# Seven block products for values and output projection, with the values exchanged through DRAM

## The chip, the cores and the metric

The kernel runs on one core of a Trainium2 chip. The metric is device time in microseconds (us) of one execution, start to end; a lower number is better.

## The reference

One transformer layer over x of shape (1, 2048, 256), all in float32:

```python
xn = _layernorm(x, axis=-1)
# attention: 16 heads of 128
qkv = einsum('bsd,ed->bse', xn, Wqkv); q, k, v = heads of qkv
w = softmax(einsum('bqhd,bkhd->bhqk', q, k) * D ** -0.5)
out = einsum('bhqk,bkhd->bqhd', w, v).reshape(B, S, H * D)
attn = einsum('bse,de->bsd', out, Wout)
# feed-forward with weights quantized to -1, 0, 1
hidden = sigmoid(xn @ q(w1).T) * (xn @ q(w2).T)
x = x + attn + hidden @ q(w3).T
```

What the change touches is two of the projections: the values v (2048 rows by 256 inputs, 128 columns for each head) and the output product with Wout (256 outputs, 128 inputs for each head).

## The kernel before

**Blocks and steps.** After a lead-in (layer norm, feed-forward part, projections of the first heads) the work is a loop over 64 blocks, 16 heads times 4 query blocks of 512 rows. Block n has 4 steps t = 0 to 3. Two heads make a group g of 8 blocks; i = n mod 8 is the place of a block in its group. Blocks with i = 0 to 3 belong to the first head of the group, those with i = 4 to 7 to the second. There are 8 groups and so 7 passages from i = 7 of one group to i = 0 of the next.

**A step on TensorE (PE).** In each step PE makes the scores of 128 query rows, six steps ahead of the block whose values it weighs (`scores`, L548), then a projection product that is fitted in ("first product", `beside`), then one part r = t of the weighted sum (`weighted`, L695), then perhaps a "second product". Queries and keys of the head after next are made in steps t = 2 and 3 by `fast_product`/`fast_read` (L163, L180): a 2 x 2 block matrix product in seven block products instead of eight, after Strassen and Winograd. Steps t = 0 and 1 hold other products: for i = 0 to 3 the output projection of the group before (`o_product`, `o_read`), for i = 4 to 7 the values of the group after (`v_product`, `v_read`). Both are plain products of eight block products' worth. All these products use the one PSUM bank of pool `ps_m`, so that each must wait until VectorE (DVE) has read the one before it.

**The weighted sum.** The softmax weights p are exchanged between rows by DMA, turned by DVE (`transposed`, L641, line L646 of the profile) into the buffer R, and weighed by the values in seven products as well. For that GpSimd (POOL) subtracts slots of R (`differences`, L651): T1 in two halves a and b, T2 in two halves l and h, T3 in two halves, T4 in one piece twice as long. It also adds and subtracts quarters of the value tile (`v_combined`, L682) once for each head: two of these before the first block of the head, and two in its step 1, ahead of T4. T1b, T2l and T2h are needed by the weighted part r = 1, T3 and the last `v_combined` by r = 2, T4 by r = 3. In step t = 2 the DVE transposes for the next block overwrite a slot that T4 reads, and so wait for T4.

**Order.** There is no scheduler: each engine takes its instructions in the order in which the program writes them. POOL also starts the DMAs that are not part of the exchange, in that same order: the result of a block goes to DRAM at the start of the next block's step 0 (`put_away`, L766), the inverse sums go out in step 2 (`rd<-r`) and come back spread over the rows in step 1 (`spread`), and `between` (L872) fetches weights, stored results (`o_fetched`) and partial sums (`y_moved`), step by step.

Of the kernel before, what the change touches and what calls it, by code (L numbers as in the profile page):

```python
# [9 lines left out]
F32 = mybir.dt.float32  # L10
# [10 lines left out]
def layernorm_attention_bitffn_kernel(  # L21
# [18 lines left out]
    D = P  # L40
# [49 lines left out]
    def in_halves(out, lhs, rhs, start, stop, both=(True, True)):  # L90

        for c in range(2):
            if both[c]:
                nc.tensor.matmul(  # L94
                    out[c * HP : (c + 1) * HP], lhs[:, c * HP : (c + 1) * HP], rhs,
                    start=start, stop=stop, skip_group_check=True,
                )
# [47 lines left out]
    def weight_sums(h: int):  # L145
# [6 lines left out]
        nc.gpsimd.tensor_tensor(w[:, 3], wk[:, 1], w[:, 1], sub)  # L152
        ws[h] = w

    def x_sums(c: int):
        t = apool.tile([P, 4, QB], F32, tag=f"t{c}", name=f"t{c}", bufs=1)
        x00, x10 = (xnT[:, d, bass.ts(c, QB)] for d in range(KC))
        x01, x11 = (xnT[:, d, bass.ts(c + 1, QB)] for d in range(KC))
        for i, (a, b) in enumerate(((x01, x00), (x11, t[:, 0]), (x11, x01), (x10, t[:, 1]))):
            nc.gpsimd.tensor_tensor(t[:, i], a, b, ALU.subtract)  # L160
        ts[c] = t

    def fast_product(h: int, b: int, i: int, second: bool):  # L163

        c = b // 2 * 2
        wk, wq = (weights[h // G, i][:, :, bass.ts(h % G, D)] for i in "kq")
        w, t = ws[h], ts[c]
        x00, x10 = (xnT[:, d, bass.ts(c, QB)] for d in range(KC))
        x11 = xnT[:, 1, bass.ts(c + 1, QB)]
        lhs, rhs = {  # L170
            (0, 0): ((wk[:, 0], x00), (w[:, 1], t[:, 1])),
            (0, 1): ((w[:, 2], t[:, 2]), (wq[:, 1], t[:, 3])),
            (1, 0): ((w[:, 0], t[:, 0]), (w[:, 3], x11)),
            (1, 1): ((wk[:, 1], x10),),
        }[b % 2, i][second]
        pm = ps_m.tile([P, QB], F32, tag="m", name=f"pw{h}_{b}_{i}_{int(second)}")
        in_halves(pm, lhs, rhs, True, True)
        return pm

    def fast_read(h: int, b: int, i: int, second: bool, pm):  # L180
        c = b // 2 * 2
        if (b % 2, i) == (0, 0):
            if not second:
                if c == 0:
                    kTs[h] = kvpool.tile([P, S], F32, tag="kT", name=f"kT{h}")
                for j in range(2):
                    qTs[h, c + j] = kvpool.tile(
                        [P, QB], F32, tag="qT", name=f"qT{h}_{c + j}", bufs=NB + 2
                    )
        k0, k1 = (  # L190
            kTs[h].rearrange("p (j k r) -> p k j r", j=P // 32, r=32)[:, j * TB : (j + 1) * TB]
            for j in (c, c + 1)
        )
        q0, q1 = qTs[h, c], qTs[h, c + 1]
        pk = pm.rearrange("p (k j r) -> p k j r", j=P // 32, r=32)
        def q_sum(q, base):
            nc.vector.tensor_tensor(q, pm, base, ALU.add)

        def k_sum(k, base):
            nc.vector.tensor_tensor(k, pk, base, ALU.add)  # L200

        if (b % 2, i) == (0, 0):
            if not second:
                nc.vector.tensor_copy(k0, pk)
            else:
                k_sum(k1, k0)
        elif (b % 2, i) == (0, 1):
            if not second:
                nc.vector.tensor_tensor(
                    q1.rearrange("p (k j r) -> p k j r", j=P // 32, r=32), pk, k1, ALU.add  # L210
                )
            else:
                q_sum(q0, q1)
        elif (b % 2, i) == (1, 0):
            if not second:
                q_sum(q1, q1)
            k_sum(k1, k1)
        else:
            k_sum(k0, k0)
# [1 line left out]
    NV = NKT // 2  # L221

    osums = const.tile([P, 2, DM // P, QB], F32, tag="osums", name="osums")
    o3 = const.tile([P, G, QB], F32, tag="o3", name="o3")
    rinvs = [
        [const.tile([P, 32], F32, tag=f"r{i}{j}", name=f"r{i}{j}") for j in range(2)]
        for i in range(2)
# [30 lines left out]

    def v_product(g: int, m: int, second: bool):
        w = weights[g, "v"]
        pm = ps_m.tile([P, 2, G * D], F32, tag="m", name=f"pvw{g}_{m}")
        for j in range(2):
            for d in range(KC):
                in_halves(
                    pm[:, j], xnT[:, d, bass.ts(2 * m + j, P)], w[:, d], d == 0, d == KC - 1
                )
        return pm

    def v_read(g: int, m: int, second: bool, pm):
        for j in range(G):
            nc.vector.tensor_copy(
                v_tile(g * G + j)[:, 2 * m : 2 * m + 2], pm[:, :, bass.ts(j, D)]
            )

    ppool = ctx.enter_context(tc.tile_pool(name="ppool", bufs=2))
    front = ExitStack()
# [7 lines left out]
    ods = [  # L286
        [away.tile([P, G, QB], F32, tag=f"od{g}_{c}", name=f"od{g}_{c}") for c in range(NB)]
        for g in range(2)
    ]
    rds = [away.tile([P, 32], F32, tag=f"rd{i}", name=f"rd{i}") for i in range(2)]  # L290

# [481 lines left out]

    def o_fetched(g: int, b: int):
        nc.gpsimd.dma_start(o3, ods[g % 2][b])

    def y_moved(b: int, back: bool):
        y, yd = osums[:, (b + 1) % 2], yds[b]  # L780
        nc.gpsimd.dma_start(*((yd, y) if back else (y, yd)))

    def o_product(g: int, m: int, second: bool):
        w = weights[g, "o"]
        pm = ps_m.tile([P, QB], F32, tag="m", name=f"pow{g}_{m}")
        for i in range(G):
            in_halves(pm, w[:, i, bass.ts(m % 2, P)], o3[:, i], i == 0, i == G - 1)
        return pm

    def o_read(g: int, m: int, second: bool, pm):  # L790
        b, e = divmod(m, 2)
        y = osums[:, (b + 1) % 2, e]
        to = xnT[:, e, bass.ts(b, QB)] if g == H // G - 2 and b > 1 else y
        nc.vector.tensor_tensor(to, pm, y, ALU.add)

    sofar = {}

# [74 lines left out]
    def between(n: int, t: int):  # L872

        g, i = divmod(n, GB)
        last = NBK - NB

        if t == 1:
            if i == NB - 1 and g + 1 < H // G:
                load_weights(g + 1, "v", nc.gpsimd)
            elif i == GB - 1 and n < last or n == last - 1:  # L880
                load_weights(g, "o", nc.gpsimd)
        if g and i < NB:
            if t == 0 and i + 1 < NB:
                y_moved(i + 1, False)
            elif t == 1 and i + 1 < NB:
                o_fetched(g - 1, i + 1)
        elif n < last:
            if (i, t) == ((GB - 2, 2) if g else (GB - 1, 2)):
                y_moved(0, False)
            if (i, t) == (GB - 2, 3):  # L890
                o_fetched(g, 0)
        if n >= last - 1 and t == 2:
            b = n + 1 - last
            nc.gpsimd.dma_start(o3[:, b % 2], ods[(H - 2) // G % 2][b][:, 0])
        if (n, t) in ((last - 2, 3), (last - 1, 0)):
            fetched_back(n + 2 - last)
        if t == 0 and n in (last - 3, last - 2, last, last + 1):
            x_fetched((last - 3, last - 2, last, last + 1).index(n))

    behind = []  # L900
    with tc.manual_schedule():
        for u in range(-LEAD, (NBK - 1) * TB):
# [13 lines left out]
            if n >= NB and t < 2:  # L916
                i, j = divmod(i, NB)
                j = 2 * j + t
                if not i:
                    seven, hi = True, (g - 1, j)  # L920
                    product, read, twice = o_product, o_read, False
                elif g + 1 < H // G:
                    seven, hi = True, (g + 1, j)
                    product, read, twice = v_product, v_read, False
            pms = []

            def beside():
# [10 lines left out]
            if t == 0 and n >= 0:  # L938
                if 0 < n <= NBK - NB:
                    put_away(n - 1)  # L940
                differences(n, "T1b")
            elif t == 1 and n >= 0:
                differences(n, "T2h")
                differences(n, "T3b")
                spread(n)
                if blocks[n][1] == 0:
                    v_combined(blocks[n][0], 2)
                    v_combined(blocks[n][0], 3)
                differences(n, "T4")
            elif t == 3 and -1 <= n < NBK - 2:  # L950
                differences(n + 1, "T1a")
                if n % GB < NB <= n < NBK - NB - 2:
                    y_moved(n % GB, True)
                differences(n + 1, "T3a")
                if n >= 0 and blocks[n + 1][1] == 0:
                    v_combined(blocks[n + 1][0], 0)
                    v_combined(blocks[n + 1][0], 1)
            if more:
# [117 lines left out]
```

## Time and profile before

| | before |
|---|---|
| time, median of 3 runs | 2169.45 us (2166.16 to 2170.13) |
| time of the profiled execution | 2168.17 us |
| its span, first to last instruction | 2166.4 us |
| PE / DVE / ACT / POOL busy | 99% / 80% / 64% / 68% |
| granted TensorE clock | full speed throughout |
| DMA engines busy, mean rate | about 55%, 139 GB/s |

All line numbers in profile lines are those of the kernel before. `128*64` is a matmul on half the columns of the array; a float32 matmul shows as two records, so 16 records of 128x512 are four pairs of matmuls. A wait is put down to what ended last. Idle time of an engine that is not the bottleneck costs nothing.

### The profile page before, as it was taken

Reading aid. Unit: us, or ns where it says so; the run is one execution under the profiler, and the core shown is the slowest. Engines: PE = TensorE matmul, PEld = TensorE weight load, DVE = VectorE, ACT = ScalarE, POOL = GpSimd, SP = SyncE. Lnnn points to the kernel's source line nnn. Section 1 sums busy time; section 2 is a strip of 40 time slices with the busy share of each in tenths; the row PEclk is TensorE's granted clock in tenths of the full one; section 3 lists DMA queues with packets and bytes.
Section 4 is the critical chain, followed back from the end, with each engine's and each line's share of the span. In section 5 each row is a group of like instructions: output and inputs, shape, how many; then the busy total and the mean of one; then the engine's idle time right before and its main releaser. Section 6 shows DMA issues by size and latency. Waiting matters only on the chain. (4 is left out here: it accounts for less than half of the span.)

```text
span 2166.4 us, 41304 instructions
## 1 busy us (share of the span) xinstructions
PE 2153.8 (99%) x14074; PEld 1068.8 (49%) x14074; DVE 1726.9 (80%) x2338; ACT 1378.8 (64%) x2414; POOL 1474.5 (68%) x884
## 2 busy tenths in 40 slices
PE   9999999999999999999999999999999999999999
PEld 6744445444544444444444444544444444544456
DVE  6577887887887787887788788788788788788785
ACT  5587766666666666666666666666666666666673
POOL 0067767867667767767767776777766777676873
PEclk9999999999999999999999999999999999999999
DMA  2155555665556655566555654656555665556653
GB/s 94 40 117 140 130 121 126 166 178 128 115 141 165 162 129 125 143 171 154 124 133 144 169 149 110 145 154 169 135 116 135 169 162 132 117 145 176 178 143 98
DMA packets 180771, 300.65 MB, mean 139 GB/s; under 512 B 54416, under 2 KB 59920, under 8 KB 180560
## 3 DMA queue, kind: packets, MB, share of 16 engines
q1 hardware_dynamic: 127856, 175.21, 32.1%
q0 software_dynamic: 27152, 88.30, 16.6%
q10 hardware_dynamic: 25552, 34.51, 6.3%
q8 instruction: 111, 1.82, 0.4%
q14 instruction: 100, 0.82, 0.1%
HBM read 61.93 MB, written 34.54 MB: 45 GB/s over the span
## 5 line engine op out<-in xcount | busy, mean ns | idle before, releaser
L666 POOL TENSOR_TENSOR R<-R 128x1024 f32<-128x1024 f32 x441 | 1177.3, 2679 | 184.8 <-DVE R L646 103.9
L94 PE MATMUL s<-kT,qT 128*64 128x512 f32 x4000 | 901.1, 592 | 0.8 <-ACT p L578 0.8
L602 ACT COPY part<-p 32x512 f32<-32x512 f32 x1024 | 632.4, 618 | 380.9 <-issue 271.0
L568 DVE TENSOR_REDUCE mx<-s 128x1 f32<-128x1024 f32 x512 | 620.0, 1222 | 291.7 <-PE s L94 278.2
L578 ACT ACTIVATE p<-s,nm 128x1024 f32<-128x1024 f32 x512 | 567.0, 1112 | 212.4 <-PE pw L94 115.9
L646 DVE STREAM_TRANSPOSE R<-part 128x1024 f32<-128x1024 f32 x512 | 605.2, 1221 | 15.8 <-DMA part<-p 13.3
L94 PEld LDWEIGHTS s<-kT,qT 128*64 128x64 f32 x4000 | 288.2, 137 | 500.9 <-issue 440.8
L713 PE MATMUL av<-R,v 128*64 128x256 f32 x3728 | 528.5, 379 | 1.4 <-DVE oU L739 1.3
L713 PE MATMUL av<-R,st 128*64 128x256 f32 x3024 | 456.2, 379 | 2.5 <-DVE oU L739 1.6
L713 PEld LDWEIGHTS av<-R,v 128*64 128x64 f32 x3728 | 326.2, 137 | 141.0 <-issue 46.0
L713 PEld LDWEIGHTS av<-R,st 128*64 128x64 f32 x3024 | 283.5, 137 | 187.7 <-issue 55.2
L731 ACT COPY oU<-av 64x256 f32<-64x256 f32 x248 | 91.2, 368 | 121.2 <-PE av L713 118.7
L769 POOL DMA_DIRECT2D od<-oU x60 | 34.1, 568 | 184.8 <-DVE oU L743 184.5
L617 POOL DMA_DIRECT2D rd<-r x60 | 33.9, 564 | 169.0 <-DVE r L616 169.0
L739 DVE TENSOR_TENSOR oU<-av,oU 64x256 f32<-64x256 f32 x248 | 102.1, 412 | 44.7 <-ACT oU L731 42.1
L94 PE MATMUL pvw<-wv,xnT 128*64 128x256 f32 x896 | 106.2, 379 | 0.0
L94 PE MATMUL pow<-o,wo 128*64 128x512 f32 x448 | 105.6, 592 | 0.0
L578 ACT ACTIVATION_READ_ACCUMULATOR p<-s,nm 128x1 f32 x512 | 100.7, 197 | 0.0
L94 PEld LDWEIGHTS pvw<-wv,xnT 128*64 128x64 f32 x896 | 64.3, 137 | 56.3 <-issue 26.7
L94 PE MATMUL pw<-t,ws 128*64 128x512 f32 x336 | 86.4, 592 | 0.0
L200 DVE TENSOR_TENSOR kT<-pw,kT 128x512 f32<-128x512 f32 x112 | 76.9, 687 | 1.8
L160 POOL TENSOR_TENSOR t<-xnT 128x512 f32<-128x512 f32 x4 | 5.1, 1271 | 106.8 <-DMA part<-p 106.8
(146 smaller groups left out, 1295.1 us busy)
## 6 DMA issues: line engine op xcount, KB each, us to landing
part<-p SPq DMA_DIRECT2D x2560, 64.0 KB, 2.2
part<-p ACTq DMA_DIRECT2D x512, 64.0 KB, 2.2
oT<-rd POOLq DMA_DIRECT2D x60, 256.0 KB, 5.6
od<-oU POOLq DMA_DIRECT2D x60, 256.0 KB, 2.7
o<-od POOLq DMA_DIRECT2D x28, 512.0 KB, 4.4
osums<-yd POOLq DMA_DIRECT2D x28, 512.0 KB, 4.5
yd<-osums POOLq DMA_DIRECT2D x26, 512.0 KB, 3.4
yd<-yT SPq DMA_DIRECT2D x4, 512.0 KB, 2.6
```

What stands on the lines that cost most here:

```text
L94: nc.tensor.matmul(out[c * HP : (c + 1) * HP], lhs[:, c * HP : (c + 1) * HP], rhs, start=start, stop=stop, skip_group_check=True,)
L200: nc.vector.tensor_tensor(k, pk, base, ALU.add)
L568: nc.vector.tensor_reduce(mx[:, i : i + 1], s, AX.X, ALU.max)
L578: nc.scalar.activation(p, s, AF.Exp, bias=nm, scale=SCALE, accum_out=sums[n][:, t, i : i + 1],)
L602: nc.scalar.copy(*ends(j, j))
L617: nc.gpsimd.dma_start(rds[n % 2], riT)
L646: nc.vector.transpose(to[:, t % 2, 2 * i : 2 * i + 2], part.rearrange("p g (s c) -> p g s c", s=2),)
L666: nc.gpsimd.tensor_tensor(o, x, y, ALU.subtract)
L713: nc.tensor.matmul(av[i * HP : (i + 1) * HP, half], l[:, kk], moving(s, kk), start=start, stop=(k == units[r] - 1), skip_group_check=True,)
L731: nc.scalar.copy(u[op, oq], av[ap, half])
L739: nc.vector.tensor_tensor(u[p, q], av[p, half], u[p, q], ALU.add)
L769: nc.gpsimd.dma_start(ods[h // G % 2][b][:, h % G], oU)
```

## The change

The values of a group (both heads) and its output projection are now each made in seven block products for two query blocks, not eight. 

For the values the moving operand is x (with the sums in `ts` that queries and keys already use), so each product gives the values with their 128 columns on the partitions, and not the keys. The results are gathered in the value tile itself and then put in order: four DMAs for each half of each head write them to DRAM (`v_sent`), one DMA reads them back (`v_landed`) into a part of `xnT` that is not read any more, and two DVE transposes write the value tile (`v_transposed`). To free that part, the second pair of x blocks takes its two blocks in the other order (`pair`).

For the output the product that follows is added in PSUM onto the one before it; DVE adds the bank to the partial sums after each. `o3` has three slots, fetched one head and block at a time, with differences between them by POOL.

Weight sums for both are made by POOL (`v_sums`, `o_sums`). The products are split over the first and second product of steps 0 and 1. Only the core of the diff is shown.

```diff
+    def pair(c: int):
+        return (c, c + 1) if c == 0 else (c + 1, c)
...
-    o3 = const.tile([P, G, QB], F32, tag="o3", name="o3")
+    o3 = const.tile([P, 3, QB], F32, tag="o3", name="o3")
...
-    def v_product(g: int, m: int, second: bool):
-    def v_read(g: int, m: int, second: bool, pm):
...
+    def v_sums(g: int):
+        wv = weights[g, "v"]
+        sums_of(wv[:, :, D:], wv[:, :, :D], f"wvs{g}")
+    def sums_of(k, q, name: str):
+        w = wpool.tile([P, 4, D], F32, tag="wx", name=name)
+        nc.gpsimd.tensor_tensor(w[:, 0], q[:, 0], q[:, 1], ALU.add)
+        nc.gpsimd.tensor_tensor(w[:, 1], w[:, 0], k[:, 0], ALU.subtract)
+        nc.gpsimd.tensor_tensor(w[:, 2], k[:, 0], q[:, 0], ALU.subtract)
+        nc.gpsimd.tensor_tensor(w[:, 3], k[:, 1], w[:, 1], ALU.subtract)
+    def fast_v_product(g: int, m: int, second: bool):
...
+        lhs, rhs = (
+            ((wv[:, 0, D:], x00), (w[:, 1], t[:, 1])),
+            ((w[:, 2], t[:, 2]), (wv[:, 1, :D], t[:, 3])),
+            ((w[:, 0], t[:, 0]), (w[:, 3], x11)),
+            ((wv[:, 1, D:], x10),),
+        )[m][second]
+        pm = ps_m.tile([P, QB], F32, tag="m", name=f"pvw{g}_{half}_{m}_{int(second)}")
+        in_halves(pm, lhs, rhs, True, True)
+    def fast_v_read(g: int, m: int, second: bool, pm):
...
+        if (m, second) == (0, False):
+            nc.vector.tensor_copy(k0, pm)
+            return
+        todo = {
+            (0, True): ((k1, k0),), (1, False): ((q1, k1),), (1, True): ((q0, q1),),
+            (2, False): ((q1, q1), (k1, k1)), (2, True): ((k1, k1),), (3, False): ((k0, k0),),
+        }[m, second]
+        for o, i in todo:
+            nc.vector.tensor_tensor(o, pm, i, ALU.add)
+    def v_sent(h: int, half: int):
+        v = v_half(h, half).rearrange("p k d -> p (k d)")
+        vd = vds[h % G][half].rearrange("(j r) (q c) -> q r j c", r=32, c=S // 8)
+        for q in range(P // 32):
+            nc.gpsimd.dma_start(vd[q], v[bass.ts(q, 32)].rearrange("r (j c) -> r j c", c=S // 8))
+    def v_landed(h: int, half: int):
+        nc.gpsimd.dma_start(landing, vds[h % G][half])
+    def v_transposed(h: int, half: int):
...
+        for u in range(2):
+            nc.vector.transpose(v[:, 2 * u : 2 * u + 2], w[:, 2 * u : 2 * u + 2])
+    wxs, landing = {}, xnT[:, 0, QB : 3 * QB]
...
+    def o_fetched(g: int, b: int, head: int, slot: int):
+        nc.gpsimd.dma_start(o3[:, slot], ods[g % 2][b][:, head])
+    def o_difference(slot: int, x: int, y: int):
+        nc.gpsimd.tensor_tensor(o3[:, slot], o3[:, x], o3[:, y], ALU.subtract)
...
     def o_product(g: int, m: int, second: bool):
+        w, s = weights[g, "o"], wxs[f"wos{g}"]
+        lhs, slot, start = (
+            ((w[:, 0, :P], 0, True), (s[:, 1], 2, False)),
+            ((s[:, 0], 1, False),),
+            ((s[:, 2], 0, True), (w[:, 1, P:], 2, False)),
+            ((w[:, 1, :P], 1, True), (s[:, 3], 0, True)),
+        )[m % NB][second]
+        if start:
+            opms[g] = ps_m.tile([P, QB], F32, tag="m", name=f"pow{g}_{m}_{int(second)}")
+        in_halves(opms[g], lhs, o3[:, slot], start, True)
...
     def between(n: int, t: int):
+        v_steps = {
+            (5, 1): [(v_sent, 0, 0)],
+            (5, 3): [(v_transposed, 0, 0), (v_sent, 1, 0)],
+            (6, 1): [(v_landed, 1, 0)], (6, 2): [(v_transposed, 1, 0)],
+            (7, 1): [(v_sent, 0, 1)], (7, 3): [(v_transposed, 0, 1)],
+            (8, 1): [(v_sent, 1, 1)], (8, 3): [(v_landed, 1, 1)], (9, 1): [(v_transposed, 1, 1)],
+        }
...
+        if t == 3 and i == GB - 1 and g + 1 < H // G:
+            v_combined((g + 1) * G, 0)
+            v_combined((g + 1) * G, 1)
+        if n < last and (i, t) == (GB - 1, 3):
+            o_sums(g)
...
             elif t == 1 and n >= 0:
                 differences(n, "T2h")
+                if n >= NB and n % GB < NB and n % 2 == 0 and n < NBK - NB:
+                    o_difference(0, 2, 0)
                 differences(n, "T3b")
...
             elif t == 3 and -1 <= n < NBK - 2:
                 differences(n + 1, "T1a")
...
+                if n >= 0 and n % GB in (5, 7) and n // GB + 1 < H // G:
+                    v_landed((n // GB + 1) * G, n % GB // 2 - 2)
                 differences(n + 1, "T3a")
-                if n >= 0 and blocks[n + 1][1] == 0:
+                if n >= 0 and (n + 1) % GB == NB:
                     v_combined(blocks[n + 1][0], 0)
                     v_combined(blocks[n + 1][0], 1)
```

The keys (i, t) of `v_steps` are a block's place in its group (8 and 9 are places 0 and 1 of the group after) and its step; the numbers after a name are the head in the group and the half of the keys. `o_moved` (not shown) lays the fetches and differences of `o3` over the steps of i = 0 to 3: a partial sum for the second block of a pair is now fetched in step 0 of the first block, and the weights of the values are loaded in step 2 instead of step 1.

## The prediction

> **What bounds the kernel now.** I read the page's busy times first, then the groups by line, then the waits, then the timelines of PE, DVE and POOL around two places where the change puts its new steps.
>
> ```profile
> PE 2153.8 (99%) x14074; PEld 1068.8 (49%) x14074; DVE 1726.9 (80%) x2338; ACT 1378.8 (64%) x2414; POOL 1474.5 (68%) x884
> L94 PE MATMUL pvw<-wv,xnT 128*64 128x256 f32 x896 | 106.2, 379 | 0.0
> L94 PE MATMUL pow<-o,wo 128*64 128x512 f32 x448 | 105.6, 592 | 0.0
> ```
>
> PE has no gaps, so time is what PE is fed, as long as nobody makes it wait. The two groups are the products that the change cuts by an eighth. The others have slack that is cut up by waits:
>
> ```profile
> POOL od L769 <- DVE oU L743: 184.5, 59, 4.5
> POOL rd L617 <- DVE r L616: 169.0, 57, 13.0
> POOL R L666 <- DVE R L646: 103.9, 62, 3.6
> PE av L713 <- DVE oU L739: 2.9, 4, 1.1
> ```
>
> POOL's slack, about 3 us before `put_away` and 3 us before `rd`, takes extra work only if that work stands just there and is not itself late.
>
> **PE's saving.** The PE timeline around a passage from i=7 to i=0 (start, length, instruction):
>
> ```profile
> 1416.48 3.60 PE L94 MATMUL s<-kT,qT 128*64 128x512 f32 x16
> 1419.91 1.89 PE L94 MATMUL pow<-o,wo 128*64 128x512 f32 x8
> 1425.08 3.60 PE L94 MATMUL s<-kT,qT 128*64 128x512 f32 x16
> 1430.23 3.62 PE L713 MATMUL av<-R,st 128*64 128x256 f32 x32
> 1433.68 3.60 PE L94 MATMUL s<-kT,qT 128*64 128x512 f32 x16
> 1437.12 1.03 PE L94 MATMUL pw<-xnT,wk 128*64 128x512 f32 x4
> ```
>
> From start to start, 8 such records take 1.72 us and 4 take 0.86. Per group and kind there were 8 products of 1.72 (eight steps); now there are 14 half ones, so two times 0.86 go: in steps (0,1) and (2,1) for the output, (5,1) and (7,1) for the values, written (i,t). Saved: 2 x 2 x 7 x 0.86 = 24.0 us. All other steps keep their PE time.
>
> **DVE's added work.** Reads of the output go from 56 to 112 at 0.69 us, of the values from 112 copies at 0.42 to 112 instructions at 0.69: +39 and +30 us. 56 transposes of 512 columns, half of the L646 row (1.22 for 1024) plus a start, 0.65 each: +36. DVE goes to about 1832 us, still under PE. The reads lie in idle time: a second read comes at the start of the next step, where DVE waits 0.9 us (step 1) or 2.2 us (step 2) for scores; a double read in a first product leaves 1 us before PE's second product. Cost 0; without that cover each would cost up to 0.69.
>
> **POOL's added work.** 56 differences at 1.28 = 72 us, 56 weight sums at 0.45 = 25, and 182 more DMA issues at 0.57 = 104: about 200 us, POOL then at 77%. Most stands in the two waits above. The `o3` differences of i=1, 2 and 6 precede `put_away` (idle 4 us); the four `v_sent` issues (2.3 us) of (5,1), (7,1) precede `rd`, where POOL idles 3 to 4 us; `v_sums` pushes `put_away` by 0.9 us in i=3, where T2l then starts 0.1 us later. All 0. The later load of wv lands before its sums. The added wait in `o_product`, that a product adds to the bank that DVE has read, is the old one-bank wait: read done 1422.8, second product 1424.2. Two places are not free.
>
> **Place one: the passage i=7 to i=0** (7 times). POOL before:
>
> ```profile
> 1411.22 4.80 POOL L666 TENSOR_TENSOR R<-R 128x1024 f32<-128x1024 f32 x2 [1.64 <-DVE R L646]
> 1415.99 1.28 POOL L688 TENSOR_TENSOR st<-v 128x512 f32<-128x512 f32 x1
> 1419.94 0.57 POOL L769 DMA_DIRECT2D od<-oU  x1 [1.32 <-DVE oU L743]
> 1423.69 2.38 POOL L666 TENSOR_TENSOR R<-R 128x1024 f32<-128x1024 f32 x1 [0.78 <-PE av L713]
> 1426.01 0.56 POOL L781 DMA_DIRECT2D osums<-yd  x1
> 1434.49 4.53 POOL L666 TENSOR_TENSOR R<-R 128x2048 f32<-128x2048 f32 x1
> ```
>
> `st<-v` started at 1416.0. Now it reads values that `v_transposed` writes in the same step. That stands behind DVE's L646 pair (ends 1418.5) and needs `v_landed`, issued after T1a at 1413.6. At the 4.4 us of a like DMA that is 1418.0, so DVE is last: transposes done 1419.8. Then POOL in order, from rows: two `st` 2.64 to 1422.5; four weight sums 1.75 to 1424.3 (new); `put_away` 0.59; T1b 2.36; T2l 2.34 to 1429.6; the fetch of `osums` 0.57; T2h 2.35 to 1432.5; the new `o3` difference 1.28; T3b 2.35; `spread` 0.81; two `v_combined` 2.5 to 1439.4; T4 4.53 to 1443.96. It was at 1439.0.
>
> PE: its weighted part of step 1 would start at 1429.4 (product halved) and reach T2h's slices at 1431.1: waits 1.4. Part 2 needs the last `v_combined`: waits 1.0. Then DVE, in step 2, waits for T4: L646 from 1444.05 to 1446.3, L739 to 1447.2, the second read to 1447.9, so PE's first product of step 3 waits 0.7; two maxima and the scale to 1450.3, first read to 1451.0, second product 1451.1, end of step 3 at 1451.96. Unhindered it ends at 1449.16 - 0.86 = 1448.3. Loss 3.66 us (the waits of 1.4, 1.0, 0.7 and 0.6 lie inside it), x 7 = 25.6. The new fetch of `osums` for step 1 (landing 4.5) reaches DVE at 1434.6 against 1431.3, ahead of the T4 wait: adds nothing.
>
> **Place two: step (6,2).** `v_landed` of (6,1) stands behind T4, the weight sums of queries and a fetch. POOL's timeline, DVE's, and the list of DMA issues with the time to landing last:
>
> ```profile
> 1366.90 4.57 POOL L666 TENSOR_TENSOR R<-R 128x2048 f32<-128x2048 f32 x1
> 1372.79 0.46 POOL L152 TENSOR_TENSOR ws<-wk,ws 128x128 f32<-128x128 f32 x1
> ```
> ```profile
> 1375.40 2.37 DVE L646 STREAM_TRANSPOSE R<-part 128x1024 f32<-128x1024 f32 x2
> ```
> ```profile
> o<-od POOLq DMA_DIRECT2D x28, 512.0 KB, 4.4
> wq<-in_wqkvT_dram POOLq DMA_DIRECT2D x7, 256.0 KB, 5.6
> wk<-in_wqkvT_dram POOLq DMA_DIRECT2D x7, 256.0 KB, 4.3
> ```
>
> The transposes of (5,3) put `put_away` 1.2 us later, a fetch stands in step 0, so T4 ends near 1372.4, sums 1374.2, fetch 1374.75, then `v_landed`. DVE is free for its transposes at 1377.7. At 4.4 us it lands at 1379.15. It is queued right behind another fetch, as wq is and wk is not (5.6 against 4.3), half as long here, so up to 0.65 more. DVE then loses 1.5 to 2.1 us plus 1.3 of transposes, of which about 1.3 is slack; behind it are L739, the second read and the maxima, so PE's products of step 3 wait 1.5 to 2.1. I take 1.8 x 7 = 12.6; at the shortest `o` landing (3.3) it is 0.4 x 7 = 3, at the longest of `osums` (6.0) 3.1 x 7 = 22. At (5,3) landing and DVE meet (1418.0 against 1418.5) and PE has 0.1 us left: 0. At (9,1) DVE has 2.2 us: 0.
>
> The Trainium skill (DMA: Bandwidth & Descriptors, Anatomy of one DMA) gives a DMA from POOL's queue 2.0 us plus its bytes over 436 GB/s, 3.2 us for 512 KB; the trace says 4.4 and decides; by the rule place two would cost near 3 us. The skill also has a rule against the change (SBUF — State Buffer, the "DVE blocks DMA" trap): a DVE copy between SBUF places can keep POOL from writing descriptors, 3.1 us for a DMA of 0.62. Were each issue of a `v_sent` held so, four would overrun the idle before `rd` by some 8 us. Here 60 `od` issues all took 547 to 582 ns beside a DVE that is busy 80%, so I count 0.57.
>
> **Sum.** On the profiled execution of 2168.2 us: - 24.0 + 25.6 + 12.6 = 2182.4. The median of the runs shown stands 1.3 us above that execution: 2183.7, given as 2184.
>
> **Rivals.**
> 1. *PE's saving reaches the end (faster).* It needs T4 of i=0 done by 1440.3, that is POOL's chain from `st` shorter by 3.7 us, and `v_landed` of (6,1) by 1377.7. For it: POOL is only 77% busy, and DVE has idle time at other steps. Against it: each link of the chain is an in-order row. If half of the chain's loss and none of place two remains: 2169.5 - 24.0 + 12.8 = 2158; none of it, 2145.5. Chance 0.20.
> 2. *The passage costs what I say and place two nothing (no change).* Landings at 3.3 us and a POOL that catches up: 2169.5 - 24.0 + 25.6 = 2171. Chance 0.13.
> 3. *Landings get slower under the added transfers (slower still).* At 5.5 us, the longest `o` landing, (5,3) and the passage wait 0.6 more and place two 0.8 more: 2.0 x 7 = +14, 2198. At 6.5: 2215. For it: part of the exchange shares these engines, 55% busy. Against: the change adds 29 MB to 301. Chance 0.09.
> 4. *DVE becomes the bound.* 1832 us over 64 blocks is 28.6 of a block's 32; against. It would show as waits in every block, 0.5 x 56 = 28: 2212. Chance 0.03.
>
> The forecast has 0.55, its own range 2174 to 2194. The range for 8 in 10 goes down into rival 1 and up to rival 3: 2156 to 2204. A difference within 0.2%, 4.3 us, can't be told from none. Faster 0.20 (rival 1), same 0.13 (rival 2), slower 0.67 (the forecast and rivals 3 and 4).
>
> **What would show it.** Right: PE's `pvw` and `pow` groups shrink by an eighth; PE idle of about 5 us a group, waiting in part 1 and 2 for POOL (R, st) and in products of step 3 for DVE, at i=0 and i=6 only; DVE R L646's successor waiting for POOL T4 at i=0, and DVE `v<-xnT` waiting for a DMA at (6,2). Wrong: PE idle under 2 us a group (rival 1), `xnT<-vd` landing well off 4.4 us (rivals 2, 3), or waits spread over all i (rival 4).

## The result, and the profile after

| | before | after |
|---|---|---|
| time, median | 2169.45 us (2166.16 to 2170.13) | 2196.65 us (2196.33 to 2204.99) |
| ratio to before | | 1.0142, 95% interval 1.0126 to 1.0159 |
| profiled execution, its span | 2168.17, 2166.4 us | 2196.33, 2194.4 us |
| PE / DVE / ACT / POOL busy | 99 / 80 / 64 / 68% | 98 / 83 / 63 / 76% |
| granted TensorE clock, profiled execution | 1.000 | 0.999 |

The change costs 27 us, where the forecast had 14.5. Line numbers moved by 67 for most lines: the exchange's transposes are L713 now (L646 before), POOL's differences of R L733 (L666), the sums of value quarters L755 (L688), the weighted sum's matmuls L780 (L713 before), the reads of its result L806 (L739) and L810 (L743), `put_away` L836 (L769), `o_read` L880 (L794), `o_fetched` L844 (L777), `y_moved` L851 (L781). New are L326 (`v_sent`), L329 (`v_landed`), L335 (`v_transposed`), L847 (difference of `o3`), and L273 to L276 (weight sums).

The page's busy times, and from the groups by line the products of values and output (`line engine op out<-in x count | busy, mean ns | idle before`):

```profile
PE 2147.7 (98%) x13514; PEld 1110.2 (51%) x13514; DVE 1818.1 (83%) x2450; ACT 1375.0 (63%) x2414; POOL 1670.8 (76%) x1178
```
```profile
L94 PE MATMUL pow<-o,wos 128*64 128x512 f32 x224 | 59.1, 598 | 7.2 <-DVE osums L880 6.7 <-DVE qT L202 0.3
L94 PE MATMUL pow<-o,wo 128*64 128x512 f32 x168 | 43.5, 592 | 0.0
```

The two `pow` groups have 392 records where there were 448: an eighth is gone. Their busy time fell by 3 us only (105.6 to 102.6), since a run of four records shows 1.03 us where the next thing starts after 0.86, and there are now 98 such runs for 56. What PE really needs is read from start to start.

The waits of the kernel after (`engine line waited for: us in total, times, longest us`) have lines that the waits of before did not have at all:

```profile
POOL st L755 <- DVE v L335: 23.8, 7, 4.3
DVE osums L880 <- DMA osums<-yd: 36.7, 16, 4.7
DVE R L713 <- POOL R L733: 16.2, 7, 2.8
PE pw L94 <- DVE kT L205: 15.3, 13, 4.0
DVE v L335 <- DMA xnT<-vd: 12.9, 8, 2.3
PE pow L94 <- DVE osums L880: 6.7, 12, 1.1
PE av L780 <- POOL st L755: 3.9, 7, 0.6
```

Counts of 7 are the seven passages. PE's three lines make 25.9 us; at which steps it loses them, this view does not say. I cut PE's timeline at the first matmul of each step's scores and took the mean of each step (i,t) over the six groups that lie whole inside the loop, after minus before:

| step | after - before, us | | step | after - before, us |
|---|---|---|---|---|
| (0,0) | +0.92 | | (2,1), (5,1), (7,1) | -0.86 to -0.87 each |
| (0,1) | -0.32 = -0.86 + 0.54 | | (2,0) | +0.55 |
| (0,2) | +1.20 | | (6,0) | +0.27 |
| (0,3) | +1.14 | | (6,3) | +3.02 |
| | | | (1,0) | +0.15 |

All other steps agree to 0.02 us, which leaves no room for a cause that acts on all steps alike, such as the clock. The sum is +4.3 a group; seven such groups are 30, and the profiled executions differ by 28.2.

**The passage.** PE, DVE and POOL in the timeline of after, at the longest of the six passages (its four steps lose 4.74 us, those of the others 3.59 to 3.67); step (0,0) starts at 1431.50, (0,1) at 1441.93, (0,2) at 1450.23, (0,3) at 1460.03 (columns: start, length, instruction, idle time before it and what ended it):

```profile
1436.29 3.67 PE L780 MATMUL av<-R,v 128*64 128x256 f32 x32 [0.33 <-DVE oU L806]
1441.05 1.08 PE L94 MATMUL pow<-o,wos 128*64 128x512 f32 x4 [1.09 <-DVE osums L880]
1448.88 1.73 PE L780 MATMUL av<-R,st 128*64 128x256 f32 x13 [0.33 <-POOL R L733]
1455.67 0.43 PE L780 MATMUL av<-R,st 128*64 128x256 f32 x1 [0.56 <-POOL st L755]
1464.05 1.08 PE L94 MATMUL pw<-t,ws 128*64 128x512 f32 x4 [0.41 <-DVE kT L205]
```
```profile
1434.47 1.30 DVE L335 STREAM_TRANSPOSE v<-xnT 128x512 f32<-128x512 f32 x2 [1.00 <-DMA xnT<-vd]
1436.27 1.41 DVE L810 TENSOR_TENSOR oU<-oU,oT 128x512 f32<-128x512 f32 x1
1460.15 2.37 DVE L713 STREAM_TRANSPOSE R<-part 128x1024 f32<-128x1024 f32 x2 [2.54 <-POOL R L733]
```
```profile
1435.86 1.26 POOL L755 TENSOR_TENSOR st<-v 128x512 f32<-128x512 f32 x1 [4.34 <-DVE v L335]
1437.21 1.61 POOL L755 TENSOR_TENSOR st<-st,v 128x512 f32<-128x512 f32 x1
1438.78 0.45 POOL L273 TENSOR_TENSOR wos<-wo 128x128 f32<-128x128 f32 x1
1440.53 0.58 POOL L836 DMA_DIRECT2D od<-oU  x1
1455.57 4.55 POOL L733 TENSOR_TENSOR R<-R 128x2048 f32<-128x2048 f32 x1
```

POOL idles 4.34 us for the transposed values, then makes `st`, then the weight sums, and only then `put_away`; from there on it has no gap until T4 ends at 1460.1. DVE's exchange waits 2.54 us for that, and PE's `pw` in step (0,3) waits for DVE behind it: this is the chain that the prediction wrote down.

**Step (6,2).** POOL and DVE:

```profile
1387.83 0.55 POOL L844 DMA_DIRECT2D o<-od  x1
1388.38 0.53 POOL L329 DMA_DIRECT2D xnT<-vd  x1
```
```profile
1393.68 1.30 DVE L335 STREAM_TRANSPOSE v<-xnT 128x512 f32<-128x512 f32 x2 [2.33 <-DMA xnT<-vd]
```

The read-back is issued right behind a fetch and DVE can use it 5.30 us after its issue.

### The profile page after: what moved, and what is told of

It is laid out like the page before. It is cut to its first block, busy times and chain, and to the rows that moved or that the text cites. A ratio compares the mean times of both kernels' runs of the same rounds, so it can differ in the third digit from the quotient of the medians.

```text
span 2194.4 us, 40651 instructions
## 1 busy us (share of the span) xinstructions
PE 2147.7 (98%) x13514; PEld 1110.2 (51%) x13514; DVE 1818.1 (83%) x2450; ACT 1375.0 (63%) x2414; POOL 1670.8 (76%) x1178
## 5 line engine op out<-in xcount | busy, mean ns | idle before, releaser
L733 POOL TENSOR_TENSOR R<-R 128x1024 f32<-128x1024 f32 x441 | 1177.7, 2678 | 109.5 <-DVE R L713 71.6
L713 DVE STREAM_TRANSPOSE R<-part 128x1024 f32<-128x1024 f32 x512 | 605.0, 1220 | 36.8 <-DMA part<-p 19.1
L94 PEld LDWEIGHTS s<-kT,qT 128*64 128x64 f32 x4000 | 316.9, 137 | 509.8 <-issue 474.8
L780 PE MATMUL av<-R,v 128*64 128x256 f32 x3728 | 531.7, 380 | 2.2 <-DVE oU L806 1.8
L780 PE MATMUL av<-R,st 128*64 128x256 f32 x3024 | 461.9, 379 | 8.5 <-POOL st L755 3.9
L780 PEld LDWEIGHTS av<-R,v 128*64 128x64 f32 x3728 | 342.6, 137 | 137.5 <-issue 56.3
L780 PEld LDWEIGHTS av<-R,st 128*64 128x64 f32 x3024 | 299.5, 137 | 182.5 <-issue 60.3
L836 POOL DMA_DIRECT2D od<-oU x60 | 34.0, 567 | 122.9 <-DVE oU L810 122.9
L806 DVE TENSOR_TENSOR oU<-av,oU 64x256 f32<-64x256 f32 x248 | 101.4, 409 | 14.5 <-ACT oU L798 11.7
L880 DVE TENSOR_TENSOR osums<-pow,osums 128x512 f32<-128x512 f32 x108 | 72.2, 679 | 42.1 <-DMA osums<-yd 36.7
L319 DVE TENSOR_TENSOR v<-pvw,v 128x512 f32<-128x512 f32 x98 | 65.3, 679 | 11.5 <-PE pvw L94 11.5
L847 POOL TENSOR_TENSOR o<-o 128x512 f32<-128x512 f32 x56 | 73.8, 1318 | 1.2
```

The costliest lines, as they stand in the source:

```text
L94: nc.tensor.matmul(out[c * HP : (c + 1) * HP], lhs[:, c * HP : (c + 1) * HP], rhs, start=start, stop=stop, skip_group_check=True,)
L713: nc.vector.transpose(to[:, t % 2, 2 * i : 2 * i + 2], part.rearrange("p g (s c) -> p g s c", s=2),)
L733: nc.gpsimd.tensor_tensor(o, x, y, ALU.subtract)
L780: nc.tensor.matmul(av[i * HP : (i + 1) * HP, half], l[:, kk], moving(s, kk), start=start, stop=(k == units[r] - 1), skip_group_check=True,)
L806: nc.vector.tensor_tensor(u[p, q], av[p, half], u[p, q], ALU.add)
L847: nc.gpsimd.tensor_tensor(o3[:, slot], o3[:, x], o3[:, y], ALU.subtract)
```

## The experiments

Theory A, the prediction's: the losses stand at single places of the in-order engines, the passage and step (6,2), and each goes when its place is mended. Theory B: the added work (more DMAs, a busier DVE and POOL) slows everything, so that mending a place brings little. Theory C came up later: the passage has too much work in any order.

### 1. The output part alone

From the changed kernel, the values back to the plain product and no exchange:

```diff
-                    product, read, twice = fast_v_product, fast_v_read, j % NB != NB - 1
+                    product, read, twice = v_product, v_read, False
...
-        v_steps = {(5, 1): [(v_sent, 0, 0)], ...}
+        v_steps = {}
```

> Only the output's part of the change: seven products with sums in PSUM, three slots; the values are made as before, no exchange through DRAM. Theory A (three in-order places): PE saves 12.0 us; POOL's chain at the passage i=7 to i=0 is longer than before by the weight sums (1.75) and one difference (1.28) but starts from values that are long there, so T4 ends at 1440.1 on the scale of the prediction, inside DVE's slack: 0 lost there, nothing at step (6,2); the late fetch of the partial sums for step (2,0) still costs 0.55 a group. So -12 + 4 = about 2161 us, faster than before. Theory B (the added work and transfers slow everything in proportion): half of the 52 us that were lost come with this half, -12 + 26 = about 2183.

Measured 2158.87 us (2156.98 to 2160.95), ratio 0.9956 (0.9940 to 0.9973). Steps (0,1) and (2,1) are 0.86 shorter, (2,0) 0.23 longer, nothing else moved: half of the change is faster.

### 2. The values alone

The output as before, the values in seven products:

```diff
-                    product, read, twice = o_product, o_read, j % NB != 1
+                    product, read, twice = o_product, o_read, False
...
-            o_sums(g)
```

> Only the values' part: seven products, exchange through DRAM; the output's products as before. Theory A: PE saves 12.0 us; at the passage the chain from the transposed values to T4 lacks the weight sums and the difference (3.0 us), so T4 comes 0.9 us after DVE wants to go on, within its slack of 1.3: near 0 lost; at step (6,2) the landing is issued 1.1 us earlier than in the changed kernel and not behind a fetch, so that about 0.8 a group is lost instead of 3.0; (6,0) 0.3. So -12 + 8 = about 2165 us. Theory B: half of the 52 us and more, since the transfers are in this half: 2183 or above.

Measured 2162.49 us (2158.66 to 2167.33), ratio 0.9975 (0.9965 to 0.9986). Steps (5,1) and (7,1) are 0.86 shorter, (6,3) 0.75 and (6,0) 0.11 longer; the passage loses nothing. So the parts alone bring -8.9 and -5.3 us and both together +27. What makes the loss is that they meet.

### 3. The read-back of (6,1) one step earlier

```diff
-            (6, 1): [(v_landed, 1, 0)], (6, 2): [(v_transposed, 1, 0)],
+            (6, 0): [(v_landed, 1, 0)], (6, 2): [(v_transposed, 1, 0)],
```

> The changed kernel with one DMA moved: the read back of the first half of the group's second head is issued in step (6,0), right after T2l, instead of step (6,1), behind T4, the weight sums and a fetch. Theory A: the landing is 12 us earlier, DVE finds it there, and step (6,3) falls from 9.9 to 6.9 us: 3.0 x 7 = 21 us less than the changed kernel, about 2175. Theory B: the same transfers and the same work, so the time moves by less than 5 us: 2192 or more.

Measured 2177.78 us (2176.62 to 2178.26), ratio 1.0042 (1.0027 to 1.0057). Step (6,3) is back at 6.88 us, the passage's loss is as it was. One DMA issue, moved by a step, is worth 19 us.

### 4. The passage's POOL work in another order

The output's weight sums go ahead of the values' sums, where POOL waits for DVE anyway, and one difference goes behind T4:

```diff
+        if n < last and (i, t) == (GB - 1, 3):
+            o_sums(g)
         if t == 3 and i == GB - 1 and g + 1 < H // G:
             v_combined((g + 1) * G, 0)
             v_combined((g + 1) * G, 1)
-        if n < last and (i, t) == (GB - 1, 3):
-            o_sums(g)
...
-                    o_difference(0, 2, 0)
                 differences(n, "T3b")
...
                 differences(n, "T4")
+                    o_difference(0, 2, 0)
```

> The changed kernel with two moves in POOL's order: at the passage the four weight sums of the output stand before the two value sums that wait for DVE (POOL idles 4.3 us there), and the difference between T2h and T3b stands behind T4. Nothing is left out. Theory A: T2h comes 1.75 us earlier and T4 3.0 us earlier, so of the 3.8 us lost at the passage the parts in steps (0,1), (0,2), (0,3) go (0.54 + 1.20 + 1.14) and the 0.9 of step (0,0) stays: 2.9 x 7 = 20 us less than the changed kernel, about 2176. Theory B: the same work in another order, less than 5 us: 2192 or more.

Measured 2182.23 us (2176.36 to 2191.73), ratio 1.0066 (1.0047 to 1.0085). The losses of (0,1), (0,2) and (0,3) are gone, (0,0) keeps 1.1, and 0.52 are new at (1,0) (see the last section); (6,3) keeps 2.94. That is 6 us short of what I expected. What is new at (1,0) and (0,0), 0.37 and 0.19 us a group more than in the kernel after, makes 3.9 of the 6; the six runs lie between 2176 and 2192 us, so that the rest can't be told from their spread.

### 5. Partial sums fetched one step earlier

```diff
         elif (a, t) == (1, 2):
             if more:
+                y_moved(b + 2, False)
...
         elif (a, t) == (1, 3) and more:
-            y_moved(b + 2, False)
```

> The changed kernel with one DMA moved: the partial sums of block 2 are fetched in step (1,2), ahead of the fetches of stored results, instead of step (1,3). Theory A: DVE's first read of step (2,0) no longer waits for them (1.9 us in the trace of the changed kernel), and PE's second product of that step loses nothing: 0.55 x 7 = 4 us less than the changed kernel, about 2193, with step (2,0) at 8.6 us. Theory B (general slowing): no difference, 2197.

Measured 2191.77 us (2187.87 to 2196.50), ratio 1.0112 (1.0099 to 1.0126). The 0.55 us at (2,0) are gone. They were a wait that the prediction did not have. In the kernel after, the fetch is issued at 1238.10, right behind the load of `wk`, and DVE waits for it until 1245.09 (POOL, then DVE):

```profile
1237.36 0.75 POOL L83 DMA_DIRECT2D wk<-in_wqkvT_dram  x1
1238.10 0.55 POOL L851 DMA_DIRECT2D osums<-yd  x1
```

```profile
1245.09 0.69 DVE L880 TENSOR_TENSOR osums<-pow,osums 128x512 f32<-128x512 f32 x1 [1.86 <-DMA osums<-yd]
```

In the kernel after, the six fetches of partial sums that stand behind `wk` land 5.74 to 6.89 us after their issue, 6.60 in the mean; the other 22 land after 4.63 in the mean. Step (2,0) loses 0.74 to 0.78 us in the three groups where that landing takes 6.83 to 6.89, 0.51 and 0.54 where it takes 6.65 and 6.64, and nothing at 5.74.

### 6. The read-back ahead of the fetch

Only the order of the two DMA issues in (6,1) is swapped:

```diff
-            (6, 1): [(v_landed, 1, 0)], (6, 2): [(v_transposed, 1, 0)],
+            (6, 2): [(v_transposed, 1, 0)],
...
             if i == GB - 2:
                 if t < 3:
+                    if t == 1 and g + 1 < H // G:
+                        v_landed((g + 1) * G + 1, 0)
                     o_fetched(g, *((0, 0, 0), (1, 0, 1), (1, 1, 2))[t])
```

> The changed kernel with two DMAs of step (6,1) in the other order: the read back first, then the fetch of a stored result. It is issued only 0.55 us earlier. Theory A1 (what is queued right ahead of it on POOL's queue makes the landing slow): it lands in about 4.8 us instead of 5.8, DVE waits 1.5 us less, and step (6,3) loses 1.5 instead of 3.0: 10 us less than the changed kernel, about 2186. Theory A2 (the landing is slow there for all the other transfers around it): only the 0.55 us are won, 4 us less, about 2193.

Measured 2181.66 us (2180.84 to 2182.70), ratio 1.0065 (1.0051 to 1.0079). POOL and DVE at (6,2):

```profile
1379.84 0.55 POOL L329 DMA_DIRECT2D xnT<-vd  x1
1380.39 0.54 POOL L844 DMA_DIRECT2D o<-od  x1
```
```profile
1384.05 1.30 DVE L335 STREAM_TRANSPOSE v<-xnT 128x512 f32<-128x512 f32 x2 [0.67 <-DMA xnT<-vd]
```

From issue to use it is 4.21 us here and 4.47 in the mean of the seven places, against 5.64 in the kernel after. So 0.55 us of the gain is the earlier issue and 1.2 the place in the queue, more than A1 had for both; (6,3) loses 0.98 instead of 3.02. This is not one lucky execution: in experiments 4, 5 and 8, which leave these two issues as they were, the mean from issue to use is 5.58, 5.77 and 6.21 us.

### 7. Four moves together

The moves of 3 and 5, the weight sums of 4, and in steps (5,3) and (7,3) `v_landed` ahead of T1a and `v_transposed` ahead of the exchange's transposes:

```diff
+                if n >= 0 and n % GB in (5, 7) and n // GB + 1 < H // G:
+                    v_landed((n // GB + 1) * G, n % GB // 2 - 2)
                 differences(n + 1, "T1a")
...
+            if t == 3 and n >= 0 and n % GB in (5, 7) and n // GB + 1 < H // G:
+                v_transposed((n // GB + 1) * G, n % GB // 2 - 2)
             if v > 1 and v - 2 < NBK * TB - 2:
                 transposed(v - 2)
```

> The changed kernel with four moves and nothing left out: the read back of (6,1) in (6,0); the weight sums of the output ahead of the value sums at the passage; the partial sums of block 2 in (1,2); and in steps (5,3) and (7,3) the read back ahead of T1a and its transposes ahead of DVE's exchange transposes. Theory A: POOL's chain at the passage begins 2.4 us earlier and is 1.75 shorter, so that T4 ends at 1439.9 on the prediction's scale, inside the slack; places one and two and step (2,0) cost nothing, and of PE's 24.0 us nearly all reaches the end, less 2 us for rests in steps (0,0) and (6,0): about 2147, faster than before by 1.0%. Theory B: the added work itself slows the kernel: above 2180.

Measured 2159.39 us (2156.92 to 2160.46), ratio 0.9961 (0.9949 to 0.9974). It beats both kernels, but by less than half of what I expected: 1.7 us a group are left at (0,0) and (0,3), 0.2 at (1,0).

### 8. Values' sums behind put_away

```diff
-        if t == 3 and i == GB - 1 and g + 1 < H // G:
-            v_combined((g + 1) * G, 0)
-            v_combined((g + 1) * G, 1)
...
                     put_away(n - 1)
+                if n and n % GB == 0:
+                    v_combined(blocks[n][0], 0)
+                    v_combined(blocks[n][0], 1)
```

> The changed kernel with POOL's two value sums at the passage moved behind the store of the block's result, so that POOL waits for DVE's scaling of that result (a DVE add with two SBUF inputs) instead of running beside it. If that scaling takes 1.41 us there, and 0.69 in every other block, because a POOL operation runs at that moment, it is back at 0.69 and step (0,0) loses 0.2 instead of 0.9; the chain behind is some 0.9 us shorter, since the weight sums fill POOL's wait: 1.6 x 7 = 11 us less than the changed kernel, about 2186. If the length has another cause, it stays at 1.41 and step (0,0) at 9.4: 6 us less, 2190.

Measured 2193.92 us (2191.20 to 2197.09), ratio 1.0120 (1.0105 to 1.0136): 3 us less than the changed kernel, a smaller gain than either figure. L810 takes 0.69 us at all seven passages again and (0,0) loses 0.28 instead of 0.92, so its length did come from the POOL operation beside it (see the last section). But the chain behind `put_away` is longer by the two sums, and (0,1) to (0,3) lose what they lost; and (6,3), where nothing was changed, loses 3.53 us a group in this execution, 0.5 more than in the kernel after.

### 9 and 10. Better places for the sums

Four moves, with the transposes of (5,3) and (7,3) behind L713 again and the two sums behind T1b; and the same with the difference behind T4.

```diff
                 differences(n, "T1b")
+                if n and n % GB == 0:
+                    v_combined(blocks[n][0], 0)
+                    v_combined(blocks[n][0], 1)
```

> This is the kernel of four moves with two of its places changed: the exchange's transposes of steps (5,3) and (7,3) stand behind DVE's L713 pair again, and the two sums of the values at the passage stand on POOL behind put_away and T1b, no longer ahead of them. Theory A (every loss is one in-order place): step (0,0), which lost 1.36 us there, loses nothing, since DVE no longer waits for the landing with the pair behind it, L810 takes 0.69 us and put_away is not held by the sums; T2l comes 2.6 us later, which PE's second step still covers; step (0,3) keeps 0.2 to 0.4 us. Sum: 2159.4 - 7 x 1.4 = 2150, down to 2148 if (0,3) ends too. Rival C (DVE and POOL together have too much to do at the passage, whatever the order): the loss of 1.4 to 1.9 us a group only moves, to step (0,1) or (0,3), and the time stays at 2159.

> As the kernel with the values' sums behind T1b, and the output's difference of steps (i,1), i even, stands behind T4. Theory A: T4 ends 1.3 us sooner at i=0, so (0,3) loses nothing; but at (1,0) the difference can come late, 0.2 to 0.5 us as in the run that moved it alone. Sum 2147 to 2151, level with the other within 3 us. Rival C: 2159, as the other.

Measured 2168.72 us (2164.09 to 2173.25), ratio 1.0001 (0.9993 to 1.0010), and 2162.15 us (2159.95 to 2164.37), ratio 0.9975 (0.9965 to 0.9985). Neither A's nor C's number holds for the first: it is 9 us slower than with four moves. POOL shows why (the first line is `put_away`, the second T4 of the same passage):

```profile
1421.27 0.57 POOL L836 DMA_DIRECT2D od<-oU  x1 [3.40 <-DVE oU L810]
1438.76 4.55 POOL L733 TENSOR_TENSOR R<-R 128x2048 f32<-128x2048 f32 x1
```

The sums had stood in a gap, and the gap stayed (3.40 us) while they went into the chain that has none: T4 ends 22.0 us after `put_away` starts, with four moves 19.6. In the second, T4 ends 1.45 us sooner than in the first, but (1,0) loses 0.58, and the passage keeps 1.70 us, 1.00 of it in (0,3); its time is nearer to C's 2159 than to A's 2147 to 2151.

### 11. Five moves: four, and the late difference

The difference of steps (i,1) goes behind T4, as in 4.

> The kernel of four moves, and also the output's difference of steps (i,1), i even, behind T4. In the runs so far the loss of steps (0,0) to (0,3) is the end of T4, counted from the start of step (0,0), less 23.9 us (before 22.55, output alone 23.89, changed kernel 27.69, four moves 25.57). Theory A, with that rule: T4 ends 1.28 us sooner than with four moves, at 24.3; the loss falls from 1.69 to 0.4 us a group. The late difference costs 0.5 at (1,0), since POOL's next difference then lies beside DVE's L810, which then takes 1.4 us, not 0.7. Per group - 3.46 + 0.4 + 0.5 = -2.5, times 7: 2167.9 - 18 = 2150. Rival C (the passage has too much work in any order): no better than four moves, 2159.

Measured 2157.68 us (2154.41 to 2160.68), ratio 0.9955 (0.9941 to 0.9968), level with four moves; the 2150 did not come, and C's figure did. T4 ends at 24.92, not 24.3, and the loss of 1.91 us a group now stands in (0,0) alone, ahead of T4. DVE and PE there:

```profile
1408.64 1.30 DVE L335 STREAM_TRANSPOSE v<-xnT 128x512 f32<-128x512 f32 x2 [1.95 <-DMA xnT<-vd]
```
```profile
1412.70 3.67 PE L780 MATMUL av<-R,v 128*64 128x256 f32 x31 [1.25 <-DVE oU L806]
```

With the transposes ahead of its other work, DVE waits for the landing with everything behind it. The 0.5 expected at (1,0) did not appear.

### 12. Output alone, and one subtraction made twice

```diff
                     v_combined(blocks[n][0], 3)
+                    if n and n % GB == 0:
+                        v_combined(blocks[n][0], 3)
                 differences(n, "T4")
```

> The output part alone, with one of the values' subtractions on POOL (v_combined, the fourth, 1.27 us) made twice in step (0,1) ahead of T4, 7 times in all; the second writes the same numbers. Theory A (slack of POOL's chain up to T4 of 1.3 us, used up by the output part): T4 ends at 23.89 + 1.27 = 25.16, and all of it reaches the end, 7 x 1.27 = 8.9 us: 2158.9 + 8.9 = 2167.8. Theory B (POOL is only 73% busy and not the bound, so that one instruction more is hidden): 2159.

Measured 2168.82 us (2166.59 to 2171.72), ratio 1.0004 (0.9995 to 1.0013): 10 us more than without it, as A says, and B falls. At the passage whose step (0,3) starts at 1185.65, POOL's subtraction is double and T4 later, and DVE waits for T4 (POOL, then DVE):

```profile
1178.59 2.65 POOL L755 TENSOR_TENSOR st<-v,st 128x512 f32<-128x512 f32 x2
1181.19 4.56 POOL L733 TENSOR_TENSOR R<-R 128x2048 f32<-128x2048 f32 x1
```
```profile
1185.79 2.37 DVE L713 STREAM_TRANSPOSE R<-part 128x1024 f32<-128x1024 f32 x2 [2.73 <-POOL R L733]
```

### What they say together

The end of T4, counted from the start of step (0,0), and the loss of steps (0,0) to (0,3) against what their matmuls need, means of six passages in us:

| kernel | T4 ends | loss | T4 less loss |
|---|---|---|---|
| before | 22.55 | 0 | |
| output alone | 23.89 | 0.01 | 23.88 |
| values alone | 24.55 | 0 | |
| after | 27.69 | 3.80 | 23.89 |
| read-back one step earlier | 27.62 | 3.74 | 23.88 |
| partial sums one step earlier | 27.69 | 3.80 | 23.89 |
| read-back ahead of the fetch | 27.89 | 4.00 | 23.89 |
| values' sums behind put_away | 27.09 | 3.21 | 23.88 |
| four moves | 25.57 | 1.69 | 23.88 |
| sums behind T1b | 26.97 | 3.08 | 23.89 |
| output alone, one more subtraction | 25.26 | 1.38 | 23.88 |
| sums behind T1b, late difference | 25.52 | 1.70 | 23.82 |
| passage's POOL work in another order | 24.89 | 1.11 | 23.78 |
| five moves | 24.92 | 1.91 | 23.01 |

Where T4 decides, the passage loses exactly what T4 ends after 23.88 us (with the values alone step (0,1) is 0.86 longer, so the mark should be 24.74; no run passes it). That leaves 1.33 us of slack. The output alone adds 1.34 to the chain, the length of its one difference (1.28), and just fits; the values alone add 2.00, and fit under their own mark. Together they add 5.14: both, and the weight sums of the output, 1.8 us, which with the output alone go into POOL's waits ahead of `put_away` and T2l (1.32 and 0.78 us in before) and now stand behind the values' late sums. The last three rows are off the rule, since some or all of their loss stands ahead of T4.

Theory B falls: with the same work in another order, experiments 3 to 7 are 5 to 37 us faster than the changed kernel. Theory C stays open for the passage: every kernel with both parts keeps 1.1 to 4.0 us there, and none reaches what PE's saving alone would give (2145.5 us).

## Why the prediction was right and wrong

**Direction: right**, by its own mechanism. PE's saving was as computed: 0.86 us in each of (0,1), (2,1), (5,1) and (7,1). Rival 1 asked for T4 done by 1440.3, 23.8 us after the start of the step; the mark that the runs show is 23.88.

**Place one: right.** Forecast 3.66 us a group, measured 3.80; T4 forecast 27.48 us after the start of (0,0), measured 27.48 to 27.50 in four of the six passages. How it is spread over the steps was not right: (0,0) was to lose nothing and loses 0.92, because L810 took 1.41 us where I had 0.69 (and, in the passage shown, because the landing took 5.91 us where I had 4.4; there (0,0) lost 1.8, in the other five 0.72 to 0.79). With the values alone L810 takes 1.41 us as well and (0,0) loses nothing: there the step has no second product that waits behind it. The 0.92 does not come on top: T4 has the last word.

**Place two: the mechanism right, its size wrong.** The forecast was 1.8 us a group, the measurement 3.02. The issue came where I put it (2.9 us before step (6,3)); the term that failed is the landing, taken as 4.4, at most 5.05 us, and 5.64 us in the mean from issue to use. In the six groups DVE could use it 4.93, 6.58, 5.14, 5.30, 5.14 and 7.63 us after the issue, and step (6,3) lost 1.92, 3.66, 2.18, 2.33, 2.11 and 5.91: four lie at my upper bound and cost 2.1 as I had for it, two lie far out and make the mean. In these two the profile names another transfer of the same queue as what ended DVE's wait; but the read-back itself landed 6.4 and 7.4 us after its issue, 0.2 us before DVE began, so the late landing is its own. I had the longer landing of a DMA that is queued behind another in view (`wq` 5.6 against `wk` 4.3), and took half of it ("half as long here, so up to 0.65 more"). Experiment 6 shows 1.2 us, nearly the whole of that difference. The Trainium skill (DMA: Bandwidth & Descriptors, Two DMAs through the same engine are not ordered) states that within one queue of one DMA engine descriptors start in order but are pipelined; that fits a read-back that waits behind the fetch, though no run here shows single descriptors.

**Not in the sum at all: about 1.0 us a group.** I put POOL's other new work at "All 0" and gave the fetches that `o_moved` shifts no term, but for one at the passage. One of the others, the partial sums of (1,3), comes too late for (2,0): 0.55 us, shown by experiment 5. By the trace it is the same as at place two, a landing behind another issue of POOL's queue; no run swapped these two issues alone. At (5,3) I had the landing 0.5 us ahead of DVE, with 0.1 us left for PE, and put the step at 0; in two of six groups DVE waits 0.8 us for the landing and (6,0) loses 0.9, a mean of 0.27. (1,0) adds 0.15; in experiment 5 it loses 0.04, but its cause stays open.

Together: forecast - 3.43 + 3.66 + 1.8 = 2.03 a group, measured - 3.46 + 3.80 + 3.02 + 0.97 = 4.33. Of the 2.3 missing, 1.2 are place two and 1.0 the zeros.

**Rivals.** Rival 1 is what each part does alone, and what a reordered kernel does. Rival 2 failed at place two. Rival 3 named the right quantity, a later landing (the list of DMA issues has `xnT<-vd` at a median of 4.8 us), but not in the way that it decides. Some transfers did get slower (the exchange's `part<-p` from 2.2 to 2.6 us on SyncE's queue and 3.2 on ScalarE's, `rd<-r` from 2.0 to 3.1; the traffic grew by 33 MB, not the 29 that I had), yet the steps outside the table do not show it. `osums<-yd` went from 4.5 to 4.6 in the median, which hides the six behind `wk`. What decides are late landings at single places. Rival 4 did not come: DVE is busy 1818 us, forecast 1832, and no step outside the table moved. The sign that I named for PE's saving, `pvw` and `pow` an eighth shorter, could not be read from busy time, only from counts and steps.

## What to carry to other kernels

Two changes that each fit the slack of one in-order chain may not fit together: find the chain that sets the stage's end, measure its slack in microseconds (here 1.33 us, on an engine that is 68% busy), and add up what all parts put into it, with the work that a late input pushes out of a gap. A step on such an engine is free only in the gap where it stands. For a landing that an engine meets with little slack, take the late ones among its like, not the median, and count a DMA right behind another on its queue as late by the whole difference that the profile shows for such pairs (here 1.2 us at (6,2) and about 2 us behind `wk`).

## What the hardware showed

DVE's L810, which adds two SBUF tiles, takes 0.69 us in all blocks of before and 1.41 at the seven passages of after, where POOL's L755 runs beside it. At (1,0) of the kernel of experiment 10 it is POOL's L847:

```profile
1445.09 1.27 POOL L847 TENSOR_TENSOR o<-o 128x512 f32<-128x512 f32 x1
```
```profile
1445.53 1.38 DVE L810 TENSOR_TENSOR oU<-oU,oT 128x512 f32<-128x512 f32 x1
```

DVE's instruction ends 0.55 us after POOL's, as if it began only then. Over the traces of all fourteen kernels L810 takes 0.69 to 0.70 us in 729 of 840 cases; in the 110 cases in which it takes more than 0.75, it ends 0.545 to 0.555 us after the POOL operation that was running when it started. This fits the 0.5 and 0.6 us lost at (1,0) in experiments 4 and 10; in experiment 11 L810 takes 0.69 there and nothing is lost. In experiments 8 to 10, where no POOL sum stands beside it at the passage, it takes 0.69 there. The Trainium skill (SBUF — State Buffer, Who interferes with whom) says that a DVE instruction with two SBUF inputs and a GpSimd instruction that reads SBUF exclude each other for the whole instruction; the runs agree. The rule of the same page that the prediction weighed against this change is about DVE copies between SBUF places; the DVE copies of this loop read PSUM, so no run here tests it. The 112 issues of `v_sent` took 551 to 597 ns, 560 in the mean.
